# Layer 1 of a four-layer image network: one matrix for a patch's own pixels, filtered pixels only at patch edges, two channels side by side

## The chip, the cores and the metric

The kernel runs on one core of a Trainium2 chip. A core has TensorE for matrix products (PE in the profile, with its weight loads as PEld), VectorE (DVE), ScalarE (ACT), GpSimd (POOL) and SyncE (SP), which here does nothing but issue DMAs. The engines run their own instruction streams in order and wait for each other on semaphores. On-chip memory (SBUF) has 128 partitions; products land in PSUM banks of 128 x 512 fp32. The metric is the device time of one execution in microseconds.

## The reference

Four residual layers work on four images of 48 x 256 x 256, fp32, each after a group normalisation. Layer 1 is the one that is edited:

```python
y = jnp.einsum('oc,bchw->bohw', w_in, x)                    # 48 -> 288 channels
yp = y.reshape(B, C2, ht, P, wt, P).transpose(0, 1, 2, 4, 3, 5)
f = jnp.fft.rfft2(yp) * fft_mask[None]                      # patches of 8 x 8
yp = jnp.fft.irfft2(f, s=(P, P))
y = yp.transpose(0, 1, 2, 4, 3, 5).reshape(B, C2, H2, W2)
y = lax.conv_general_dilated(y, w_dw, ..., feature_group_count=C2)   # depthwise 3 x 3
x1, x2 = jnp.split(y, 2, axis=1)
g = jax.nn.gelu(x1, approximate=False) * x2
return jnp.einsum('oc,bchw->bohw', w_out, g)                # 144 -> 48 channels
```

Layer 0 has 1x1 and depthwise convolutions and a product of spectra; layer 2 samples an integral image at four computed corners of each pixel (gathers from DRAM); layer 3 has convolutions, a gate and a spectral filter.

## The kernel before, in words

**Two streams.** `run` interleaves two generators, a and b, by the costs that they yield (`yield 12` and so on, one unit is meant as about 1 us): the one that is behind goes on. Stream a does layers 0 and 1 of image 0, then of images 1, 2 and 3, then layer 3 of all four. Stream b does the first statistics of each image, once the weights of layer 1 (`patch_weights`, after the first statistics of image 0), and then layer 2 of image after image. Layer 2 of an image needs its layer 1. So layer 1 of image 0 runs with nothing beside it, and layer 1 of images 1 to 3 beside layer 2 of the image before. Stream a issues its DMAs on SyncE, stream b on GpSimd; layer 2's loads A and B of shifted rows go out on ScalarE. Stream a has five PSUM banks, stream b two.

**Layer 1 in three stages.** A tile of 8 x 16 pixels (two patches) is laid over the 128 partitions. The first stage makes the 288 channels and stores them in DRAM (`hD`). The second, which is edited, goes over 72 groups of four channels. The third reads the gated product (`gD`) by strips, transposes it and projects it to 48 channels.

**A group of the second stage, before.** A filter by spectrum on a tile is a 128 x 128 matrix for each channel (`cD`). The depthwise convolution is another matrix, 128 + 52 rows by 128 (`tD`): 128 rows for the tile's own pixels, 52 for the pixels of other tiles around it. `fetch` loads the next group: `hg` (pixels, 1 MB), `ct` (filter), `tt` (own rows of the depthwise matrix), `ht` (its 52 halo rows). `filtered(c)` makes the filtered pixels of a channel (L728) and ACT or DVE copies them into `ys`, four channels one behind the other, with an empty row and column around them. `gated(c)`, one group later, makes each output channel by two products into one bank: own pixels `ys` with `tt` (L741), then halo pixels `yh` with `ht` (L742, 65 rows). ACT takes the gelu of one channel and DVE multiplies it with its partner (L746). The order of products in a group is filtered 0, 1; gated 0, 2; filtered 2, 3; gated 1, 3.

The halo `yh` is gathered by eight DMAs from SBUF to SBUF (L783): for each entry of `AROUND`, some partitions of `ys`, shifted along the free dimension, go to others. Two entries have 16 partitions, two 8 and four (the corners) one. A copied partition holds four channels, 8976 bytes. `gD` is written every second group (L787). `ys` and `yh` have two buffers each, `hg` and `ct` two, `tt` and `ht` three.

The order in which SyncE issues per group is: `hg`, `ct`, `tt`, `ht` of the next group, eight copies `yh` of this group, and in every second group `gD`.

Of the kernel before, what the change touches and what calls it, by code (L numbers as in the profile page):

```python
# [8 lines left out]
F32 = mybir.dt.float32  # L9
I32 = mybir.dt.int32  # L10
AF = mybir.ActivationFunctionType
ALU = mybir.AluOpType
# [7 lines left out]
NS = 16  # L20
# [6 lines left out]
NG = 72  # L27
GROUPS = [c + 144 * h for g in range(NG) for h in range(2) for c in (2 * g, 2 * g + 1)]

YW = 17  # L30
YC = 33 * YW
Y0 = YW + 1
YL = Y0 + 4 * YC + Y0


AROUND = [
    (0, 16, 112, 1, -YW), (16, 16, 0, 1, YW), (32, 8, 15, 16, -1), (40, 8, 0, 16, 1),
    (48, 1, 127, 1, -YW - 1), (49, 1, 112, 1, -YW + 1), (50, 1, 15, 1, YW - 1), (51, 1, 0, 1, YW + 1),
]
NH = 52  # L40

NZ = 65

# [143 lines left out]
class Net:  # L189
# [430 lines left out]
    def patch_weights(self):  # L620


        nc, a = self.nc, self.a
        self.cD = self.dram.tile([NG, 128, 4, 128], F32, name="cD")[:]
        self.tD = self.dram.tile([4 * NG, (128 + NH) * 128], F32, name="tD")[:]
        with ExitStack() as ctx:
            w = ctx.enter_context(self.pool("pw", 1))
            sb = ctx.enter_context(self.pool("pb", 2))
            mask = self.filter_mask(a["L1_fft_mask"], [(0, 4 * NG)], w)
            dw = w.tile([9, 4 * NG], F32, name="dw")  # L630
            self.dma(dw[:], a["L1_w_dw"])
            for g in range(NG):
                m = sb.tile([128, 4, 128], F32, name="m", tag="m")
                for c in range(4):
                    nc.vector.tensor_scalar(
                        m[:, c, :], self.ri, mask[:, 4 * g + c : 4 * g + c + 1], None, ALU.mult
                    )
                ps = self.bank()
                nc.tensor.matmul(ps[:], self.ri, m[:].rearrange("p c k -> p (c k)"), start=True, stop=True)
                ct = sb.tile([128, 512], F32, name="ct", tag="ct")  # L640
                nc.scalar.copy(ct[:], ps[:])
                self.dma(self.cD[g].rearrange("p c k -> p (c k)"), ct[:])
                yield 3
            for q0 in range(0, (128 + NH) * 128, 4608):
                sh = sb.tile([9, 4608], F32, name="sh", tag="sh")
                self.dma(sh[:], a["c_shift"][:, q0 : q0 + 4608])
                for c0 in range(0, 4 * NG, 96):
                    tt = sb.tile([96, 4608], F32, name="tt", tag="tt")
                    for q in range(0, 4608, 512):
                        ps = self.bank()  # L650
                        nc.tensor.matmul(ps[:96, :], dw[:, c0 : c0 + 96], sh[:, q : q + 512], start=True, stop=True)
                        if q % 1024:
                            nc.vector.tensor_copy(tt[:, q : q + 512], ps[:96, :])
                        else:
                            nc.scalar.copy(tt[:, q : q + 512], ps[:96, :])
                    self.dma(self.tD[c0 : c0 + 96, q0 : q0 + 4608], tt[:])
                    yield 12

    def layer1(self, x, mr, y):
        nc, a = self.nc, self.a  # L660
# [3 lines left out]
        with ExitStack() as ctx:  # L664
            w = ctx.enter_context(self.pool("wa", 1))
            sb = ctx.enter_context(self.pool("ba", 2))
# [24 lines left out]
            for s in range(NS):  # L691
                xp = xps[s % 2]
                hs = sb.tile([128, 4 * NG, 2, 16], F32, name="hs", tag="hs")
                for b in range(16):
                    for h in range(2):
                        ps = self.bank()
                        nc.tensor.matmul(  # L697
                            ps[:, :288], xp[64 * h : 64 * h + 48, b, :], win[64 * h : 64 * h + 48],
                            start=True, stop=True,
# [11 lines left out]
        with ExitStack() as ctx:  # L711
            w = ctx.enter_context(self.pool("wb", 1))
            sb = ctx.enter_context(self.pool("bb", 2))
            ys = [w.tile([128, YL], F32, name=self.nm("ys")) for _ in range(2)]
            yhs = [w.tile([NZ, YL], F32, name=self.nm("yh")) for _ in range(2)]
            hts = [w.tile([NZ, 4, 128], F32, name=self.nm("ht")) for _ in range(3)]
            for t in ys + yhs + hts:
                nc.vector.memset(t[:], 0.0)

            pick = lambda t, k, c: t[:k, Y0 + YC * c : Y0 + YC * c + 32 * YW].rearrange(  # L720
                "p (h s b) -> p s h b", h=2, b=YW
            )[:, :, :, :16]
            order = lambda t: t.rearrange("p (s h b) -> p s h b", h=2, b=16)
            todo, gt = None, None

            def filtered(c):
                ps = self.bank()
                nc.tensor.matmul(  # L728
                    ps[:].rearrange("p (s n) -> p s n", n=32), ct[:, c, :], hg[:, :, c, :], start=True, stop=True
                )  # L730
                if c % 2:
                    nc.vector.tensor_copy(pick(yt, 128, c), order(ps[:]))  # L732
                else:
                    nc.scalar.copy(pick(yt, 128, c), order(ps[:]))

            def gated(c):
                go, yo, yho, to, ho = todo
                both = []
                for q in (c, c + 2):
                    ps = self.bank()  # L740
                    nc.tensor.matmul(order(ps[:]), to[:, q, :], pick(yo, 128, q), start=True, stop=False)  # L741
                    nc.tensor.matmul(order(ps[:]), ho[:, q, :], pick(yho, NZ, q), start=False, stop=True)  # L742
                    both.append(ps)
                gl = sb.tile([128, 512], F32, name="gl", tag="gl")
                nc.scalar.activation(gl[:], both[0][:], AF.Gelu)
                nc.vector.tensor_mul(  # L746
                    gt[:, :, 2 * (go % 2) + c, :], gl[:].rearrange("p (s n) -> p s n", n=32),
                    both[1][:].rearrange("p (s n) -> p s n", n=32),
                )


            def fetch(g):
                hg = sb.tile([128, NS, 4, 32], F32, name="hg", tag="hg")
                self.dma(hg[:].rearrange("p s c n -> p s (c n)"), hD[:, g])
                ct = sb.tile([128, 4, 128], F32, name="ct", tag="ct")
                self.dma(ct[:], self.cD[g])
                tt = sb.tile([128, 4, 128], F32, name="tt", tag="tt", bufs=3)
                ht = hts[g % 3]
                tv = self.tD[4 * g : 4 * g + 4].rearrange("c (k m) -> k c m", m=128)
                self.dma(tt[:], tv[:128])  # L760
                self.dma(ht[:NH], tv[128:])
                return hg, ct, tt, ht

            fetched = {0: fetch(0)}
            for g in range(NG + 1):
                if g < NG:
                    yt = ys[g % 2]
                    if g + 1 < NG:
                        fetched[g + 1] = fetch(g + 1)
                    hg, ct, tt, ht = fetched.pop(g)  # L770
                if todo is not None and todo[0] % 2 == 0:
                    gt = sb.tile([128, NS, 4, 32], F32, name="gt", tag="gt")
                for c in range(2):
                    if g < NG:
                        filtered(2 * c)
                        filtered(2 * c + 1)
                    if todo is not None:
                        gated(c)
                if g < NG:
                    yh = yhs[g % 2]  # L780
                    n = YL - 2 * Y0
                    for k, m, p0, dp, far in AROUND:
                        self.dma(  # L783
                            yh[k : k + m, Y0 : Y0 + n], yt[p0 : p0 + (m - 1) * dp + 1 : dp, Y0 + far : Y0 + far + n]
                        )
                if todo is not None and todo[0] % 2:
                    self.dma(gD[:, :, todo[0] // 2, :], gt[:].rearrange("p s c n -> p s (c n)"))  # L787
                todo = (g, yt, yh, tt, ht)
                yield 12
        st = self.stat.tile([CP, 129, 6], F32, name=self.nm("st"), tag="st" + self.stream, bufs=1)  # L790
        with ExitStack() as ctx:
            w = ctx.enter_context(self.pool("wc", 1))
            sb = ctx.enter_context(self.pool("bc", 2))
# [42 lines left out]
            strips, xts, last = {}, {}, None  # L836
# [535 lines left out]
```

## Time and profile before

| what | us |
|---|---|
| median of 3 runs | 20871.12 (20867.39 to 20881.85) |
| the profiled execution's own time | 20882.08 |
| its span, first to last instruction | 20880.3 |
| L728, filtered pixels: 2304 instructions, busy | 1264.4 |
| L741, own pixels: 2304, busy | 1174.1 |
| L742, halo: 2304, busy | 1163.1 |
| L732 and L734, evictions on DVE and ACT, busy | 396.7 and 346.2 |
| idle TensorE before L728, of it until `ct<-cD` | 417.5, 339.5 |
| idle TensorE before L742, of it until `yh<-ys` | 145.7, 111.6 |

A product of fp32 with 512 columns stands as two instructions, so 288 groups with four products a line give 2304. The profile records one execution; a row has an instruction's line, engine, operation, tiles and shape, how many there were, their busy time and mean, and how long the engine was idle before them and what ended that. DMAs are issued through a helper, so that they all have its line, L227, and are told apart by their tiles.

### The profile page before, as it was taken

The page shows a single profiled execution, that of the slowest core. Times are in us where ns is not written, and L with a number is a line of the kernel's source. Part 1 is how long each engine was busy: PE and PEld are TensorE (multiplying, and loading weights), DVE is VectorE, ACT ScalarE, POOL GpSimd, SP SyncE. Part 2 cuts the span into 40 slices and gives each one's busy share as a digit, 9 for nine tenths or more (in the row PEclk, how much of TensorE's full clock was granted, in tenths as well). Part 3 has the DMA queues.
Part 4 walks back from the last instruction along what each step waited for, and adds up shares of the span by engine and source line. Part 5 has one row for each costly group of instructions (what it writes and reads, how often), then busy time and mean ns, then how long its engine had stood idle before and what let it go on. Part 6 is the DMA issues. An engine that isn't in the chain of part 4 may idle for free.

```text
span 20880.3 us, 231985 instructions
## 1 busy us (share of the span) xinstructions
PE 18892.3 (90%) x79032; PEld 12001.4 (57%) x79032; DVE 10763.0 (52%) x21931; ACT 5909.3 (28%) x12275; POOL 8637.2 (41%) x8887
## 2 busy tenths in 40 slices
PE   7998798999878989998788899997888999999999
PEld 4565435666533346665433466654334787878888
DVE  4544322477765534677645447776554255555521
ACT  2333312344321123443311234433112211111111
POOL 1000000277754511777555216775552066666600
PEclk9899799999968999999689899996899999999999
DMA  4623886555588975555889755558897566666633
GB/s 114 135 55 82 233 217 194 137 132 134 132 235 230 241 207 139 130 134 127 233 230 240 219 133 130 133 127 229 236 239 225 137 150 151 158 152 160 151 76 74
DMA packets 2444896, 3440.27 MB, mean 165 GB/s; under 512 B 580102, under 2 KB 1997038, under 8 KB 2333179
## 3 DMA queue, kind: packets, MB, share of 16 engines
q1 hardware_dynamic: 1908216, 2084.50, 38.2%
q0 software_dynamic: 452560, 1110.45, 21.1%
q10 hardware_dynamic: 82944, 230.48, 4.4%
q8 instruction: 635, 10.40, 0.2%
q14 instruction: 541, 4.43, 0.1%
HBM read 2486.99 MB, written 802.77 MB: 158 GB/s over the span
## 4 chain that ended last, share of the span: by engine, by line
PE 65%; DMA 15%; DVE 7%; POOL 7%; issue 4%; SPq 1%; ACT 1%; DVEq 0%; ACTq 0%; POOLq 0%
PE ps L427 19%; POOL V L1037 7%; PE ps L947 6%; PE ps L728 5%; PE ps L435 4%; PE ps L741 4%; DMA ct<-cD 4%; PE ps L742 3%; PE ps L697 3%; PE ps L828 3%; DMA hD<-hs 2%; PE ps L1188 2%; DVE V L1050 2%; PE ps L815 1%; PE ps L966 1%
## 5 line engine op out<-in xcount | busy, mean ns | idle before, releaser
L1037 POOL DMA_INDIRECT V<-t,idx x8192 | 8227.0, 1004 | 4897.9 <-issue 2346.8
L427 PE MATMUL ps<-W,A 128*128 128x288 f32 (+1 forms) x24576 | 5547.3, 374 | 85.9 <-DMA A<-x 23.4
L427 PEld LDWEIGHTS ps<-W,A 128*128 128x128 f32 x24576 | 4281.6, 191 | 1226.6 <-issue 523.4
L227 POOL DMA_DIRECT2D X<-x x192 | 144.5, 757 | 4302.6 <-DMA x<-xt 3040.1
L1050 DVE TENSOR_TENSOR V<-V 128x1536 f32<-128x1536 f32 (+3 forms) x2048 | 1839.3, 900 | 19.2
L1048 DVE TENSOR_TENSOR V<-V,w 128x3072 f32<-128x3072 f32 x512 | 1713.3, 3346 | 35.9 <-DMA V<-t,idx 27.0
L728 PE MATMUL ps<-hg,ct 128*128 128x512 f32 x2304 | 1264.4, 676 | 417.5 <-DMA ct<-cD 339.5
L947 PE MATMUL ps<-A,W 112*96 112x512 f32 x3072 | 1544.9, 642 | 26.2 <-DVE xt L1069 21.5
L697 PE MATMUL ps<-win,xp 48*128 48x288 f32 x4096 | 1054.8, 594 | 547.9 <-DVE xp L684 232.4
L508 ACT COPY qkv<-ps 128x288 f32<-128x288 f32 x2048 | 769.9, 400 | 2641.1 <-PE ps L427 1258.4
L435 PE MATMUL ps<-W,B 58*128 58x288 f32 (+1 forms) x8192 | 1271.5, 391 | 26.1 <-DMA B<-x 13.8
L742 PE MATMUL ps<-yh,ht 65*128 65x512 f32 x2304 | 1163.1, 649 | 145.7 <-DMA yh<-ys 111.6
L531 DVE BATCH_NORM_STATS2 bs<-ps 128x6 f32<-128x96 f32 x2048 | 397.4, 251 | 1634.3 <-PE ps L529 1632.3
L741 PE MATMUL ps<-ys,tt 128*128 128x512 f32 x2304 | 1174.1, 632 | 27.6 <-DVE ys L732 25.7
L697 PEld LDWEIGHTS ps<-win,xp 48*128 48x128 f32 x4096 | 647.3, 259 | 924.3 <-ACT hs L704 291.9
L1168 DVE TENSOR_TENSOR gp<-gl,ps 128x192 f32<-128x192 f32 x1024 | 353.8, 351 | 1588.1 <-ACT gl L1167 1579.9
L728 PEld LDWEIGHTS ps<-hg,ct 128*128 128x128 f32 x2304 | 468.0, 211 | 1051.6 <-issue 949.1
L1167 ACT ACTIVATE gl<-ps 128x192 f32<-128x192 f32 x1024 | 332.7, 330 | 2529.4 <-PE ps L427 2245.4
L435 PEld LDWEIGHTS ps<-W,B 58*128 58x128 f32 x8192 | 762.4, 186 | 454.1 <-issue 346.4
L746 DVE TENSOR_TENSOR gt<-gl,ps 128x512 f32<-128x512 f32 x576 | 395.1, 687 | 1142.2 <-PE ps L742 1136.6
L947 PEld LDWEIGHTS ps<-A,W 112*96 112x96 f32 x3072 | 513.9, 176 | 731.4 <-issue 690.3
L742 PEld LDWEIGHTS ps<-yh,ht 65*128 65x128 f32 x2304 | 451.3, 199 | 794.3 <-issue 699.4
(186 smaller groups left out, 24654.4 us busy)
## 6 DMA issues: line engine op xcount, KB each, us to landing
hD<-hs SPq DMA_DIRECT2D x64, 4608.0 KB
hg<-hD SPq DMA_DIRECT2D x288, 1024.0 KB
gD<-gt SPq DMA_DIRECT2D x144, 1024.0 KB
gs<-gD SPq DMA_DIRECT2D x64, 2304.0 KB
V<-t,idx POOLq DMA_INDIRECT x8192
A<-x SPq DMA_DIRECT2D x512, 193.5 KB
xt<-x SPq DMA_DIRECT2D x256, 387.0 KB
A<-x ACTq DMA_DIRECT2D x512, 193.5 KB
```

The source lines that it names most:

```text
L427: nc.tensor.matmul(to(q, b), A[:, r + q, 128 * b + g : 128 * b + g + 128], W[:, g, :], start=b == 0 and g == 0, stop=b == 1 and g == 2,)
L435: nc.tensor.matmul(to(q, b), B[p, r // 2, 128 * b : 128 * b + 128], W[p, 3, :], start=b == 1, stop=b == 0)
L508: nc.scalar.copy(t.qkv[:, 2 * q + b, :], banks[2 * b + q][:, 0:288])
L697: nc.tensor.matmul(ps[:, :288], xp[64 * h : 64 * h + 48, b, :], win[64 * h : 64 * h + 48], start=True, stop=True,)
L728: nc.tensor.matmul(ps[:].rearrange("p (s n) -> p s n", n=32), ct[:, c, :], hg[:, :, c, :], start=True, stop=True)
L741: nc.tensor.matmul(order(ps[:]), to[:, q, :], pick(yo, 128, q), start=True, stop=False)
L742: nc.tensor.matmul(order(ps[:]), ho[:, q, :], pick(yho, NZ, q), start=False, stop=True)
L828: nc.tensor.matmul(pp[:CP, :], pr[:, q, :], got[q][:], start=q == 0, stop=q == 2)
L947: m = nc.tensor.matmul(ps[:96, :].rearrange("p (r c) -> p r c", c=256), W[: kk[g], g, :], of[: kk[g]], start=g == 0, stop=g == 3,)
L1037: nc.gpsimd.indirect_dma_start(out=V[:, k, 4 * cr : 4 * cr + 4, :].rearrange("p e c -> p (e c)"), out_offset=None, in_=table, in_offset=ba ...
L1048: self.pinned(nc.vector.tensor_mul(Vm, Vm, wm.unsqueeze(2).to_broadcast([128, 64, 48])))
L1050: nc.vector.tensor_add(V[:, :, 0:n, :], V[:, :, 0:n, :], V[:, :, n : 2 * n, :])
```

## The change

The filter and the own rows of the depthwise matrix of a channel are multiplied once, in `patch_weights`, to one 128 x 128 matrix. With it stand 52 columns of the filter (in 64), those that give the filtered pixels which other tiles need (`fD`, 4 x 192 columns a group). In the second stage `around` makes filtered pixels for these 64 columns only, two channels side by side: channel c on PSUM partitions 0 to 63 and channel c + 2 on 64 to 127, so that `ye` holds four channels in the width of two. `gated`, one group later, makes the own part straight from the unfiltered `hg` and adds the halo part, 52 rows at partition 0 or 64. Each group has four products with 64 columns, four with 128 on 128 rows and four with 128 on 52 rows. The halo copies become sixteen, half as many bytes each. `hg` and `f` have three buffers. In `patch_weights` the loop over the groups comes behind the making of `tD`, which it reads.

```diff
-YL = Y0 + 4 * YC + Y0
+YL = Y0 + 2 * YC + Y0
+NF = 128 + 64
...
+            for g in range(NG):
+                own = sb.tile([128, 4, 128], F32, name="own", tag="own")
+                self.dma(own[:], self.tD[4 * g : 4 * g + 4].rearrange("c (k m) -> k c m", m=128)[:128])
...
+                f = fs[g % 2]
+                for k, n, p0, dp, far in AROUND:
+                    nc.vector.tensor_copy(
+                        f[:, :, 128 + k : 128 + k + n], ct[:, :, p0 : p0 + (n - 1) * dp + 1 : dp]
+                    )
+                ps = self.bank()
+                for c in range(4):
+                    nc.tensor.matmul(
+                        ps[:, 128 * c : 128 * c + 128], ct[:, c, :], own[:, c, :], start=True, stop=True
+                    )
+                nc.scalar.copy(f[:, :, 0:128], ps[:].rearrange("p (c k) -> p c k", k=128))
+                self.dma(self.fD[g], f[:].rearrange("p c k -> p (c k)"))
+                yield 5
...
-            def filtered(c):
+            def around(c):
                 ps = self.bank()
-                nc.tensor.matmul(
-                    ps[:].rearrange("p (s n) -> p s n", n=32), ct[:, c, :], hg[:, :, c, :], start=True, stop=True
-                )
-                if c % 2:
-                    nc.vector.tensor_copy(pick(yt, 128, c), order(ps[:]))
+                for q in range(2):
+                    nc.tensor.matmul(
+                        strips(ps[64 * q : 64 * q + 64, :]), f[:, c + 2 * q, 128:NF], hg[:, :, c + 2 * q, :],
+                        start=True, stop=True,
+                    )
+                if c:
+                    nc.vector.tensor_copy(pick(ye, slice(0, 128), c), order(ps[:]))
...
+            def gated():
+                go, hgo, fo, yho, ho = todo
                 both = []
+                for c in range(2):
+                    both.append([self.bank() for _ in range(2)])
+                    for q in range(2):
+                        nc.tensor.matmul(
+                            strips(both[c][q][:]), fo[:, c + 2 * q, 0:128], hgo[:, :, c + 2 * q, :],
+                            start=True, stop=False,
+                        )
+                for c in range(2):
+                    for q in range(2):
+                        rows = slice(64 * q, 64 * q + NH)
+                        nc.tensor.matmul(
+                            order(both[c][q][:]), ho[rows, c, :], pick(yho, rows, c), start=False, stop=True
+                        )
...
             def fetch(g):
-                hg = sb.tile([128, NS, 4, 32], F32, name="hg", tag="hg")
+                hg = sb.tile([128, NS, 4, 32], F32, name="hg", tag="hg", bufs=3)
                 self.dma(hg[:].rearrange("p s c n -> p s (c n)"), hD[:, g])
-                ct = sb.tile([128, 4, 128], F32, name="ct", tag="ct")
-                self.dma(ct[:], self.cD[g])
-                tt = sb.tile([128, 4, 128], F32, name="tt", tag="tt", bufs=3)
+                f = sb.tile([128, 4, NF], F32, name="f", tag="f", bufs=3)
+                self.dma(f[:].rearrange("p c k -> p (c k)"), self.fD[g])
                 ht = hts[g % 3]
-                tv = self.tD[4 * g : 4 * g + 4].rearrange("c (k m) -> k c m", m=128)
-                self.dma(tt[:], tv[:128])
-                self.dma(ht[:NH], tv[128:])
+                for q in range(2):
+                    self.dma(
+                        ht[64 * q : 64 * q + NH],
+                        self.tD[4 * g + 2 * q : 4 * g + 2 * q + 2].rearrange("c (k m) -> k c m", m=128)[128:],
+                    )
...
                     for k, m, p0, dp, far in AROUND:
-                        self.dma(
-                            yh[k : k + m, Y0 : Y0 + n], yt[p0 : p0 + (m - 1) * dp + 1 : dp, Y0 + far : Y0 + far + n]
-                        )
+                        for q in (0, 64):
+                            self.dma(
+                                yh[q + k : q + k + m, Y0 : Y0 + n], ye[q + k : q + k + m, Y0 + far : Y0 + far + n]
+                            )
```

## The prediction, made before the run

> **What bounds it now.** I read the page first, its busy shares and its chain of waits:
>
> ```profile
> PE 18892.3 (90%) x79032; PEld 12001.4 (57%) x79032; DVE 10763.0 (52%) x21931; ACT 5909.3 (28%) x12275; POOL 8637.2 (41%) x8887
> ...
> PE 65%; DMA 15%; DVE 7%; POOL 7%; issue 4%; SPq 1%; ACT 1%; DVEq 0%; ACTq 0%; POOLq 0%
> ```
>
> TensorE is 90% busy and holds 65% of the chain, so fewer matmuls look like time. But 15% of the chain is DMA, and the largest DMA entry there is `ct<-cD`, in the very stage that is edited. So the stage must be read alone. The rows of `hg<-hD` begin at 2345, 6262, 10464 and 14669 us: 72 groups for each of the four images. The windows view over these stretches (us, then busy of PE, weight load, DVE, ACT, POOL; granted clock; DMA share; GB/s):
>
> ```profile
> 2345.00:3211.00 866.00, 795.67 (x1668) 331.81 (x1669) 200.81 (x285) 168.62 (x280) 0.00 (x0) 0.93 0.80 217
> 6262.00:7398.00 1136.00, 991.87 (x2287) 422.78 (x2288) 590.88 (x874) 189.55 (x312) 597.95 (x632) 0.90 0.91 238
> 10464.00:11605.00 1141.00, 989.01 (x2284) 423.49 (x2285) 589.50 (x872) 189.57 (x312) 597.91 (x632) 0.89 0.90 236
> 14669.00:15793.00 1124.00, 979.16 (x2290) 418.69 (x2291) 590.55 (x874) 189.58 (x312) 597.18 (x630) 0.91 0.91 240
> ```
>
> One group costs 12.2 us in image 0, where stream b is idle, and 16.0 us in images 1 to 3 beside layer 2 (71 steps from the first `hg` to the last); together 4267 us. The view has no column for SyncE, which only issues DMAs. Its timeline over two groups of image 0:
>
> ```profile
> 2818.84 0.45 SPq L227 DMA_DIRECT2D hg<-hD  x1
> 2819.34 0.42 SPq L227 DMA_DIRECT2D ct<-cD  x1
> 2819.86 0.38 SPq L227 DMA_DIRECT2D tt<-tD  x1
> 2820.34 0.84 SPq L227 DMA_DIRECT2D ht<-tD  x1
> 2821.28 7.46 SPq L227 DMA_DIRECT2D yh<-ys  x8
> 2828.91 0.60 SPq L227 DMA_DIRECT2D gD<-gt  x1
> 2829.61 1.88 SPq L227 DMA_DIRECT2D hg<-hD  x1
> 2831.55 1.22 SPq L227 DMA_DIRECT2D ct<-cD  x1
> 2832.86 0.59 SPq L227 DMA_DIRECT2D tt<-tD  x1
> 2833.54 0.60 SPq L227 DMA_DIRECT2D ht<-tD  x1
> 2834.24 9.23 SPq L227 DMA_DIRECT2D yh<-ys  x8
> 2843.58 0.46 SPq L227 DMA_DIRECT2D hg<-hD  x1
> ```
>
> From `hg` to `hg` this is 10.8 and 14.0 us, and SyncE is issuing in nearly all of it: 23.7 of 24.7 us. The eight `yh` copies take 7 to 9 us of each group. **SyncE's queue is as full as TensorE**, and in this stage it is the tighter of the two. What one copy costs it, by the rows of `yh`:
>
> ```profile
> L227 SPq DMA_DIRECT2D yh<-ys x2304: 554/712/2864, 2357.8 to 15812.8; - x192
> ```
>
> The median is 0.71 us, the minimum 0.55. The single rows of the trace split it by shape: 16 partitions 0.58 us, 8 partitions 0.61, one partition (a corner) 0.73. So 144 KB cost less than 9 KB: it is a price for each DMA, not for its bytes. `ct` and `tt`, 256 KB each, have medians of 0.44 and 0.39.
>
> A second rule sits on the same queue. The DMAs that SyncE and ScalarE issue share eight completion semaphores in turn, and each waits until the DMA eight places before it on its semaphore has landed. In the quiet group above `hg` lands 5.1 us after its issue, `ct` 0.7 us later, `tt` 2.2 us after that and `ht` 1.2 us after that (semaphore events); the fifth to eighth `yh` go out just behind those four landings.
>
> **The change, part by part.**
>
> *TensorE, per group.* Before: 12 products, each two instructions at some 0.445 us start to start (4 of L728 take 1.72 us in the chain), 10.7 us. After: 4 own products 3.56 us; 4 halo products on 52 rows at partitions 0 and 64, alternating; 4 products with 64 columns. For alternating row halves the trace has L435 beside L427 (start, us, what):
>
> ```profile
> 4500.08 1.24 PE L435 MATMUL ps<-W,B 58*128 58x288 f32 x8
> 4501.25 3.18 PE L427 MATMUL ps<-W,A 128*128 128x288 f32 x12
> ```
>
> 0.155 against 0.265 us each, a factor 0.585, so the halo costs 8 x 0.445 x 0.585 = 2.1 us. No row shows a column pair. Bounds: 2.1 us if it overlaps as the row halves do, 3.6 if not. The Trainium skill (TensorEngine Tiling, Theoretical Speedup) promises up to 2x for both; the clock gate page (TensorE: Matmul & The Clock Gate, The mechanism) says that weights load beside a running matmul only where the row groups differ, which speaks against the column pair. I take 3.6. Sum 9.3 us, 1.4 saved (2.9 at best). This is worth nothing unless TensorE ends the group.
>
> *DVE and ACT.* Two of four evictions of 0.69 and 0.60 us go, 1.3 us a group, not on the path (DVE 23% and ACT 19% busy in image 0). They now end early in the group, so the copies no longer wait for the last of four.
>
> *Bytes.* `ct` 256 + `tt` 256 KB become `f` 384 KB; halo weights and copies keep theirs. 128 of some 2620 KB a group go, 5%. The slow landing of `tt` (2.2 us) goes, `f` adds some 0.35 us.
>
> *SyncE.* Fetches stay four. The eight `yh` copies become sixteen of half the bytes, in the same shapes (16, 8 and 1 partitions): 8 more at 0.71 us and 0.065 us between two, **+6.2 us a group**. Here a rule is weighed. The Trainium skill (DMA: Bandwidth & Descriptors, Issuing engines are not separate DMA queues) says that a sequencer's time to start a DMA is usually small beside the DMA itself. By it only the bytes count: a group gets 5% shorter, 4267 us lose some 200. By the row, sixteen copies need 16 x 0.78 = 12.4 us of one queue, more than a whole group of image 0. The row decides.
>
> I put the issues and landings in order, image 0, from `hg` = 0. Quiet group: `f` 0.5, `ht` 1.0 and 1.5, copies 1 to 4 from 2.0 to 4.0; copy 5 waits for `hg` (5.1), 6 for `f` (6.2), 7 and 8 for the halves of `ht` (6.9, 7.5); the eight corners follow at 0.78 each from 8.2, the end at 14.5. Then `gD`, 0.7. Group after `gD`: `hg` 1.9 and `f` 1.2 us to issue, `hg` landing at 8.5, `f` 9.6, `ht` 10.3 and 11.0, corners from 11.8, end 18.1. The pair is 33.3 us against 24.7. The same reckoning gives 10.8 and 14.0 for before. With 0.2 us of semaphore instructions: **16.8 us a group, +4.6 x 72 = +331 us.**
>
> Images 1 to 3: SyncE issues for 8.9 us a group, needs some 2 us for gaps and semaphore instructions, and waits 5 us. After, issue and gaps alone are 15.5 (uninflated) to 16.4 us, against 16.0 for the whole group now. Of the waits, those for the evictions of `ys` (2.4 us: rows of L732, L728, L741 in its waits) mostly go, those for `hg`, `f` and layer 2's loads `A<-x` (1.4 us before) stay in part; I keep 1.9. **18.3 us, +2.3 x 216 = +497 us.** Bounds: 16.5 (no waits left, +108 us) and 21 (all 5 us stay, +1080).
>
> TensorE needs 9.3 us and some 4 of layer 2 there, and idles more. The next `hg` and the halo's copies come a group ahead, so no other loop closes later than SyncE's.
>
> *Weights, once, beside layer 0 of image 0,* where TensorE is 1812.6 of 1860 us busy, so nothing covers it. 72 groups x 4 products 128x128x128, two instructions each at 0.13 us (L885's size): 75 us. One more ACT copy (0.6 us) and eight small DVE copies (0.17 to 0.2 us each, by the 128x16 rows) a group lie beside TensorE. A second product now waits for ACT's copy of the first, and the load of `own` (512-byte pieces, POOL's queue, behind the previous store) comes two groups ahead. Bounds 60 and 250 us; I take 90, near the work itself.
>
> Sum: 331 + 497 + 90 = 918 on the profiled execution's 20,882 us, 21,800; the median of the runs shown is 11 us below it: **21,790 us.**
>
> **Rivals.** (a) *Faster:* the issue price halves with the bytes (deciding point: a 16-copy set under some 7 us). Then SyncE stays near 10 us and DMA bandwidth ends the group: 0.91 x 16.0 us x 3.69/3.82 = 14.1 us (a group of image 1 moves 3.82 MB in all: 118.34 MB in 31 groups from 6500 to 7000 us), with waits 14.8, in images 1 to 3 (-260), and 11.0 in image 0 (-86); with the weights 20,615. For it: DMA 0.91 busy and less of it. Against: the 9 KB copies that cost more than 144 KB. 5%. (b) *Much slower:* in images 1 to 3 TensorE, idling, is granted less clock (0.65 to 0.75 in neighbouring stretches of 500 us), layer 2's 13 us become 18 and alternate with SyncE's waits: 21 us, +1080, with 331 and 120: 22,400. 7%. (c) *No difference:* the row pairs' gain pays for the queue; needs groups of 14.1 us in images 1 to 3, under SyncE's 15.5. 2%.
>
> **Numbers.** Forecast 86%, its own range 21,400 to 22,150, from the 16.5 and 20 us of images 1 to 3. The range reaches up to (b) in part: 21,370 to 22,300. A measurement here tells 0.2% from no change. Faster 5%, within 0.2% 2%, slower 93%.
>
> **Signs.** Right: sixteen `yh` issues of 0.6 to 0.73 us, SyncE without gaps in image 0, 16 to 17 us from `hg` to `hg` there, and 17 to 20 later; lower PE share and DMA share in these windows; PE waiting for `yh` or `hg`. Wrong: `yh` issues near 0.35 us, groups under 15 us, or a loss that sits in layer 0's weights or outside the four stretches.

## The result and the profile after

The changed kernel takes 22,003.18 us (median of 4 runs, 22,000.82 to 22,034.29), the kernel before 20,869.25 us beside it (20,852.44 to 20,881.85): a ratio of 1.0544, 95% interval 1.0531 to 1.0556. It is 5.4% slower; the prediction was 21,790 us with a range of 21,370 to 22,300.

The page of the changed kernel: busy shares, then the shares of the chain that ended last.

```profile
PE 18771.7 (85%) x79608; PEld 11778.6 (54%) x79608; DVE 10615.9 (48%) x22209; ACT 5776.0 (26%) x12059; POOL 8685.0 (39%) x8959
...
PE 57%; DMA 19%; SPq 8%; DVE 6%; POOL 5%; issue 3%; ACT 1%; ACTq 0%; DVEq 0%; POOLq 0%
```

TensorE is less busy than before and holds less of the chain, 57% against 65%. SyncE's queue (SPq) holds 8% where it had 1%. The windows over the four stretches of the edited stage, with the columns as before (us; busy PE, PEld, DVE, ACT, POOL; granted clock; DMA share; GB/s):

```profile
2397.00:3598.00 1201.00, 770.09 (x1680) 258.77 (x1680) 143.95 (x209) 126.37 (x210) 0.00 (x0) 0.74 0.50 149
6670.00:8044.00 1374.00, 946.70 (x2296) 358.68 (x2296) 545.74 (x801) 147.79 (x242) 599.51 (x634) 0.76 0.67 190
11107.00:12483.00 1376.00, 954.36 (x2296) 361.46 (x2296) 545.98 (x801) 147.79 (x242) 600.32 (x635) 0.75 0.66 190
15548.00:16924.00 1376.00, 945.96 (x2296) 360.13 (x2296) 545.69 (x801) 147.78 (x242) 598.35 (x634) 0.76 0.67 189
```

Each stretch is longer, and everything in it that was nearly full has become emptier: the DMA engines went from 0.80 and 0.91 to 0.50 and 0.67 of their time, TensorE from 795.67 of 866 us to 770.09 of 1201, and the granted clock fell with it. SyncE's timeline shows what is full (start, us, what):

```profile
2805.38 0.43 SPq L227 DMA_DIRECT2D hg<-hD  x1
2805.91 0.37 SPq L227 DMA_DIRECT2D f<-fD  x1
2806.37 1.13 SPq L227 DMA_DIRECT2D ht<-tD  x2
2807.61 13.70 SPq L227 DMA_DIRECT2D yh<-ye  x16
2821.41 0.60 SPq L227 DMA_DIRECT2D gD<-gt  x1
2822.11 1.83 SPq L227 DMA_DIRECT2D hg<-hD  x1
```

From one `hg` to the next it is 16.7 us, and the row of the sixteen copies fills 13.7 of them. Such a row holds short waits between the copies as well: the copies' own durations add up to 10.8 us a group in image 0, and all issues to 13.85 of 16.92 (8.87 of 12.21 before). Most groups alternate: in the median 15.4 us, and 18.7 where `hg` stands behind `gD`. The whole time went like this (rows of `hg`, 71 steps an image, where the prediction counts 72 groups; the rest from the first products of layer 1):

| part | before, us | after, us | measured | predicted |
|---|---|---|---|---|
| stage, image 0 | 866.6 | 1201.6 | +335 | +331 |
| stage, images 1 to 3 | 3401.0 | 4126.1 | +725 | +497 |
| start, layer 0 of image 0, weights | 1982.8 | 2037.3 | +54.5 | +90 |
| all else | | | +5.5 | 0 |
| span | 20,880.3 | 22,000.5 | +1120 | +918 |

### The profile page after: what moved, and what is told of

Its sections match the earlier page's. It is cut to its first block, busy times and chain, and to the rows that moved or that the text cites. A ratio compares the mean times of both kernels' runs of the same rounds, so it can differ in the third digit from the quotient of the medians.

```text
span 22000.5 us, 235878 instructions
## 1 busy us (share of the span) xinstructions
PE 18771.7 (85%) x79608; PEld 11778.6 (54%) x79608; DVE 10615.9 (48%) x22209; ACT 5776.0 (26%) x12059; POOL 8685.0 (39%) x8959
## 4 chain that ended last, share of the span: by engine, by line
PE 57%; DMA 19%; SPq 8%; DVE 6%; POOL 5%; issue 3%; ACT 1%; ACTq 0%; DVEq 0%; POOLq 0%
PE ps L427 19%; SPq L227 8%; DMA f<-fD 7%; PE ps L977 5%; POOL V L1067 5%; PE ps L435 4%; PE ps L715 3%; PE ps L858 3%; PE ps L1218 2%; DMA ht<-tD 2%; DMA hD<-hs 2%; DMA yh<-ye 2%; PE ps L773 2%; DVE V L1080 1%; PE ps L845 1%
## 5 line engine op out<-in xcount | busy, mean ns | idle before, releaser
L751 PE MATMUL ps<-hg,f 128*64 128x512 f32 x2304 | 922.2, 928 | 1166.5 <-DMA f<-fD 1021.0
L977 PE MATMUL ps<-A,W 112*96 112x512 f32 x3072 | 1640.6, 676 | 25.7 <-DVE xt L1099 22.5
L773 PE MATMUL ps<-yh,ht 52*128 52x512 f32 x2304 | 1024.8, 807 | 673.5 <-DMA yh<-ye 599.1
L766 PE MATMUL ps<-hg,f 128*128 128x512 f32 x2304 | 1162.5, 650 | 0.0
L751 PEld LDWEIGHTS ps<-hg,f 128*64 128x64 f32 x2304 | 219.8, 192 | 1709.0 <-issue 1551.0
L773 PEld LDWEIGHTS ps<-yh,ht 52*128 52x128 f32 x2304 | 379.8, 225 | 1184.3 <-issue 905.8
L778 ACT ACTIVATE gl<-ps 128x512 f32<-128x512 f32 x576 | 344.0, 597 | 2493.9 <-PE ps L773 2481.0
L1197 ACT ACTIVATE gl<-ps 128x192 f32<-128x192 f32 x1024 | 333.4, 331 | 2532.8 <-PE ps L427 2225.4
```

The costliest lines, as they stand in the source:

```text
L751: nc.tensor.matmul(strips(ps[64 * q : 64 * q + 64, :]), f[:, c + 2 * q, 128:NF], hg[:, :, c + 2 * q, :], start=True, stop=True,)
L766: nc.tensor.matmul(strips(both[c][q][:]), fo[:, c + 2 * q, 0:128], hgo[:, :, c + 2 * q, :], start=True, stop=False,)
L773: nc.tensor.matmul(order(both[c][q][:]), ho[rows, c, :], pick(yho, rows, c), start=False, stop=True)
L977: m = nc.tensor.matmul(ps[:96, :].rearrange("p (r c) -> p r c", c=256), W[: kk[g], g, :], of[: kk[g]], start=g == 0, stop=g == 3,)
```

## The experiments

The chips were of two kinds. On one kind the kernel before takes 20,850 to 20,880 us, on the other 25,350 to 25,384. On the second kind image 0 runs like on the first (10.89 and 10.85 us a group for the last variant below, which ran on both), but all that runs beside layer 2 later is slower, also parts that nobody edited (layer 0 of image 1 took 2795 us in the first experiment below, 2169 in the profile of before). Why is open. So image 0 is compared between all runs, images 1 to 3 only within a kind.

### The kernel before, with sixteen copies

```diff
-                        self.dma(yh[k : k + m, Y0 : Y0 + n], yt[..., Y0 + far : Y0 + far + n])
+                        for i in (Y0, Y0 + n // 2):
+                            self.dma(yh[k : k + m, i : i + n // 2], yt[..., i + far : i + far + n // 2])
```

> The kernel before, with each of its eight halo copies cut in two along the channels: the same bytes, the same products, sixteen DMAs. Theory (SyncE pays for each DMA, whatever its bytes): eight more issues of some 0.69 us and gaps of 0.065, 6 us of SyncE's queue a group; image 0 goes from 12.2 to about 17 us a group, images 1 to 3 from 16.0 to about 19.5 to 20.5, the whole to about 22,100 us (21,800 to 22,300). Rival 1 (bytes and DMA bandwidth end the group) and rival 2 (the loss sits in the new products and their lower clock): both leave this kernel at about 20,870 us with groups of 12.2 and 16.0 us.

Measured: 26,196.9 us beside 25,384.39, ratio 1.032 (1.0303 to 1.0338), second kind of chip. Image 0 went from 12.2 to 18.0 us a group, 5.8 more. A line of its windows view and one of SyncE's timeline:

```profile
2354.00:3634.00 1280.00, 940.74 (x1680) 364.93 (x1680) 202.18 (x287) 169.30 (x281) 0.00 (x0) 0.80 0.54 147
```

```profile
2795.27 13.58 SPq L227 DMA_DIRECT2D yh<-ys  x16
```

The products, bytes, fetches and weights are those of the kernel before, only each copy is cut in two; the copies take 13.58 us of SyncE as in the changed kernel, TensorE's clock falls from 0.93 to 0.80, and the DMA share from 0.80 to 0.54. So doubling the number of DMAs makes the loss by itself in image 0, and both rivals fall there. The whole change loses 4.7 us a group: what else it does gives back about one. Over all images the loss is smaller than expected, 812 us where 22,100 meant some 1,230. Image 0 has 414 of them; for images 1 to 3 there is no trace of the kernel before on such a chip, so where the rest is missing stays open.

### The changed kernel, with copies an eighth as long

```diff
-                    n = YL - 2 * Y0
+                    n = (YL - 2 * Y0) // 8
```

> The changed kernel with its sixteen halo copies, each cut to an eighth of its length, which leaves out seven eighths of the halo pixels: the same number of DMAs, some 410 KB of 2.5 MB a group less. Theory (price for each DMA): the copies still cost 0.6 to 0.7 us of SyncE each; about 21,850 us (21,650 to 22,000), 16 to 17 us a group in image 0; what is gained comes from hg and f landing a little earlier in images 1 to 3. Rival (bytes): an issue falls under 0.4 us or the stage shrinks with its bytes by a sixth, under 21,300 us.

Measured: 25,786.91 us, ratio 1.0163 (1.0146 to 1.018), on the second kind of chip, so the total can't be set against the numbers expected. Image 0: 16.34 us a group against 16.92. Its timeline:

```profile
2796.09 0.48 SPq L227 DMA_DIRECT2D hg<-hD  x1
2796.67 0.36 SPq L227 DMA_DIRECT2D f<-fD  x1
2797.12 1.06 SPq L227 DMA_DIRECT2D ht<-tD  x2
2798.27 12.73 SPq L227 DMA_DIRECT2D yh<-ye  x16
```

Seven eighths of the halo's bytes are gone, and sixteen copies still take 12.73 us. In the single rows the medians of image 0 are 0.58 us for 16 partitions, 0.62 to 0.68 for 8 and 0.73 to 0.78 for a corner, to 0.01 us the same as in the full copies. Between these two lengths SyncE's price is for the DMA and its shape, not for its bytes. In images 1 to 3 the bytes may count for something: groups take 19.4 us there, and 20.6 with full copies in the order of the next but one experiment, on the same chip; no run tells the order from the bytes.

### The changed kernel, with half of the copies

```diff
-                        for q in (0, 64):
+                        for q in (0,):
```

> The changed kernel with only the eight copies of partitions 0 to 63, which leaves out the halo of channels c + 2: the same products. Theory (SyncE's queue ends the group): 5.5 to 6 us of it go in every group; image 0 about 11 us a group, images 1 to 3 about 14, the whole about 20,430 us (20,200 to 20,700), under the kernel before. Rival 1 (bandwidth): 9% of the stage's bytes go, at most 9% of its 5,330 us, not under 21,500 us. Rival 2 (the waits for hg and f end the group, not the issues): about 21,900 us.

Measured: 24,994.95 us, ratio to the kernel before 0.9854 (0.9835 to 0.9873), second kind of chip: 389 us under it where the expectation has some 440. Image 0: 11.3 us a group (11 expected). The rival of the waits falls, and with it that of bandwidth, which left the kernel some 600 us above the kernel before; the DMA engines' share in image 0 even rises from 0.50 to 0.63 though there is less to move.

### Another order of the same DMAs

```diff
                 self.dma(hg[...], hD[:, g])
+                copies(4)
                 self.dma(f[...], self.fD[g])
                 for q in range(2):
+                    copies(4)
                     self.dma(ht[64 * q : 64 * q + NH], ...)
...
+                copies(16)
```

The call of `fetch` with these lines moves behind `gated`, to where the copies are issued.

> The changed kernel with the same 20 or 21 DMAs a group in another order on SyncE: hg of the next group, four copies, f, four copies, the first half of ht, four copies, the second half, four copies; so the semaphore of hg or f comes round some 5 us after their issue and not after four quick ones. Theory (what is left of SyncE's time beside its issues, 1.8 us a group in image 0 and 4 in images 1 to 3, is waiting for the landing of hg, f and ht eight places earlier): most of these waits go, 0.5 and 1.5 us stay; about 21,370 us (21,200 to 21,600), image 0 about 15.6 and images 1 to 3 about 17 us a group. Rival (that time is for PSUM banks, layer 2's loads or DMA bandwidth, and turns up at the next instruction): 21,950 to 22,050 us.

> The changed kernel with its DMAs in the spread order, once more, since images 1 to 3 of the first time can't be set against the changed kernel on that chip. The first time gave 16.6 us a group in image 0, 0.35 less than the changed kernel where 1.3 was expected. Theory (waits for the landings of hg, f, ht fill the rest of SyncE's time in images 1 to 3): still 2 to 2.5 us a group less there, about 21,450 us on a chip like that of the result. Rival, now the likelier (the rest moves to the next instruction that needs the landing or a PSUM bank): within 0.8 us a group of the changed kernel in images 1 to 3, 21,800 to 21,980 us.

Measured: 26,001.45 us, 1.0238 (1.0221 to 1.0255), and 26,046.15, 1.0274 (1.0256 to 1.0291), both on chips of the second kind. Image 0: 16.57 us a group both times, 0.35 less than the changed kernel and not 1.3. A miss, and the timeline tells why:

```profile
2810.81 0.60 SPq L227 DMA_DIRECT2D gD<-gt  x1
2811.51 1.83 SPq L227 DMA_DIRECT2D hg<-hD  x1
2813.45 3.23 SPq L227 DMA_DIRECT2D yh<-ye  x4
2816.79 0.53 SPq L227 DMA_DIRECT2D f<-fD  x1
2817.36 5.29 SPq L227 DMA_DIRECT2D yh<-ye  x4
```

Other blocks of four copies take 2.5 to 3.2 us; the one here takes 5.29, because the eighth DMA after `hg` stands in it and waits for `hg`. By the semaphore events `hg`, issued behind `gD`, landed 9.8 us after its issue began (8.2 in the changed kernel, 5.0 there without `gD`), and the DMA eight places on was ready after 7.3. The wait for `f` is gone from SyncE's waits (52.6 us in image 0), those for `hg` rose from 70.0 to 89.0, and others took the rest: 192 us of waits in all became 181. For images 1 to 3 (20.6 us a group) there is no run of the changed kernel on such a chip, so whether the order is worth anything there stays open.

### Half of the copies on ScalarE, in both kernels

```diff
-                            self.dma(
+                            (nc.scalar if q else nc.sync).dma_start(
                                 yh[q + k : q + k + m, Y0 : Y0 + n], ye[...]
```

> The changed kernel with the eight copies to partitions 64 to 127 issued by ScalarE, the others by SyncE: same bytes, same products. Theory (SyncE's queue ends the group): SyncE issues for some 8.3 us a group in place of 14; image 0 about 11.5 us a group (11 to 12.5), images 1 to 3 3.5 to 5 us a group less than the changed kernel on the same chip, in all 1,100 to 1,400 us less than it, which is at or somewhat under the kernel before. Rival 1 (bytes): no difference from the changed kernel. Rival 2 (the copies stand before the gelu in ScalarE's order and hold up the PSUM banks): at most 500 us less than the changed kernel, TensorE waiting for banks that ScalarE frees.

In the kernel before, four of its eight go to ScalarE:

```diff
-                        self.dma(
+                        (nc.scalar if m == 8 or k in (48, 50) else nc.sync).dma_start(
                             yh[k : k + m, Y0 : Y0 + n], yt[...]
```

> The kernel before with four of its eight halo copies issued by ScalarE. Theory: SyncE is as full as TensorE in its groups, so this helps a little, until TensorE (10.7 us a group) or the DMA engines (0.91 busy in images 1 to 3) end the group: image 0 from 12.2 to about 11.2, images 1 to 3 from 16.0 to about 15.5 on the chip of the result; 100 to 250 us under the kernel before. Rival (TensorE alone bounded the kernel before): within 40 us of it, 12.2 us a group in image 0.

And the changed kernel again, beside these two:

> The changed kernel itself once more, as a yardstick for the other runs beside it, since the chip of the first experiments took 25,384 us for the kernel before, 22% longer than the chip of the result. Theory (the loss is SyncE's time in 288 groups): image 0 16.9 us a group, and on whatever chip a loss of 900 to 1,200 us in all; on a chip like that of the result 22,000 us. Rival (the loss is a share of the whole, by a lower clock): 5.4% on any chip, 1,370 us where the kernel before takes 25,384.

Measured, on one chip of the first kind: the changed kernel 21,986.31 us (1.0538, 1.0521 to 1.0556), with two queues 21,434.25 (1.028, 1.0263 to 1.0297), the kernel before with two queues 21,127.5 (1.0124, 1.0107 to 1.0141). The changed kernel gains 552 us, half of what was expected, 15.15 us a group in image 0. That is near the number of the second rival (at most 500 us), but its reason is the smaller part: TensorE waited 58.7 us for gelus in image 0, and 333.4 us for `f`. The kernel before *loses* 273 us, which neither theory had: 13.8 us a group in image 0 in place of 12.2, though SyncE issues for 5.5 us of it in place of 8.9. The waits (what waits, for what: us in total, times, longest), first of the changed kernel with two queues, then of the kernel before with two queues, both in image 0:

```profile
SPq L227 <- DMA yh<-ye: 354.9, 82, 9.9
...
ACT gl L778 <- DMA yh<-ye: 472.1, 48, 12.2
...
PE ps L751 <- DMA f<-fD: 333.4, 62, 25.8
```

```profile
SPq L227 <- DMA yh<-ys: 494.1, 135, 8.2
```

In the kernel before with two queues SyncE waits half of the stretch for landings of `yh`. The eight completion semaphores (108 to 115 in the trace) go round over the DMAs of both queues in program order, so SyncE's fetch of the next group stands behind a copy that ScalarE has yet to issue, behind its own evictions and gelus; and a gelu stands behind the copies. A new wait took the place of the issues. So the theory, put as "SyncE's issue time ends the group", was too narrow: fewer microseconds on SyncE help only if the DMAs do not come later for it. This reading rests on the waits; no run gave the two queues semaphores of their own. And as this chip was of the first kind again, the rival of the last expectation, a loss of 5.4% on any chip, was not put to the test.

### Copies for two groups at once

`ye` and `yh` hold the four channels of each of two groups and are twice as wide; every second group issues sixteen copies, and `gated` runs two groups after `around`, with four buffers of `hg`, `f` and `ht` and one of `gt`. `gD` goes out in the middle of the copies.

```diff
-                todo = (g, hg, f, yh, ht)
+                todo.append((g, hg, f, yh, ht))
...
-                if g < NG:
+                if g < NG and g % 2:
                     n = YL - 2 * Y0
                     for k, m, p0, dp, far in AROUND:
+                        if k == 32 and g > 2:
+                            self.dma(gD[:, :, (g - 2) // 2, :], gt[...])
                         for q in (0, 64):
                             self.dma(yh[q + k : q + k + m, Y0 : Y0 + n], ye[...])
```

> The changed kernel with its halo copies made for two groups at once: sixteen copies of double length in every second group, eight a group as before the change, the same bytes; gated runs two groups after around instead of one. Theory (price for each DMA): SyncE needs about 20 us for two groups and 2 to 4 of waits; image 0 about 11.2 us a group (10.5 to 12.5), images 1 to 3 3 to 5 us a group less than the changed kernel on the same chip, in all 900 to 1,400 less than it: about the kernel before or somewhat under it. Rival (bytes): no difference from the changed kernel, the copies of double length cost SyncE double.

Measured: 21,319.92 us, ratio 1.0221 (1.0204 to 1.0238), 666 under the changed kernel on that chip, less than expected: 14.5 us a group in image 0 and 16.6 in images 1 to 3. SyncE issues for 8.65 us a group but stands still for most of the rest. A copy of double length takes 0.86 us of it, not double the 0.68 of the changed kernel. SyncE's waits in image 0, and TensorE's for the copies:

```profile
SPq L227 <- DVE ye L756: 169.5, 35, 6.5
SPq L227 <- DVE gt L779: 130.0, 34, 4.5
...
PE ps L773 <- DMA yh<-ye: 305.1, 34, 9.4
```

The burst of copies waits for the second group's evictions, the halo products of two groups wait for the burst, and the next `around` stands behind them on TensorE: a loop that no queue's length shows.

### Eight strided copies

The last variant keeps all halo pixels. In each block of 64 partitions the 16 rows of an entry lie at every 4th partition, the 8 rows at every 8th and a corner once, so step times rows is 64, and one DMA with that step runs through both blocks:

```diff
 AROUND = [
-    (0, 16, 112, 1, -YW), (16, 16, 0, 1, YW), (32, 8, 15, 16, -1), ...
+    (0, 4, 16, 112, 1, -YW), (1, 4, 16, 0, 1, YW), (2, 8, 8, 15, 16, -1), ...   # k, step, m, ...
...
-NH = 52
+NH = 64
...
-                        f[:, :, 128 + k : 128 + k + n], ct[...]
+                        f[:, :, 128 + k : 128 + k + (n - 1) * step + 1 : step], ct[...]
...
-                        for q in (0, 64):
-                            self.dma(yh[q + k : q + k + m, ...], ye[q + k : q + k + m, ...])
+                        rows = slice(k, k + (2 * m - 1) * step + 1, step)
+                        self.dma(yh[rows, Y0 : Y0 + n], ye[rows, Y0 + far : Y0 + far + n])
```

The halo rows of the depthwise matrix are numbered in the same way; 12 of the 64 rows are zero.

> The changed kernel with the halo rows of each block of 64 partitions laid out in steps (16 rows every 4th, 8 rows every 8th, a corner once in 64), so that one DMA fetches the same shift for both channels of a pair: eight copies a group instead of sixteen, all halo pixels and all bytes as in the changed kernel, with 64 halo rows (12 of them zero) in place of 52. Theory (SyncE pays for each DMA): 5.5 to 6 us of its queue go in every group; image 0 about 11.5 us a group, images 1 to 3 about 14.6 (13.9 to 15.5, where the DMA engines' bandwidth begins to end the group); in all about 1,400 us less than the changed kernel, 20,560 (20,400 to 20,800) on a chip like that of the result: under the kernel before. Rival 1 (bytes or descriptors): a copy of 32 rows costs SyncE double and nothing is gained. Rival 2 (DMA bandwidth ends the group of images 1 to 3 at the 16 us of the kernel before): about 20,880, no better than it.

> The changed kernel with eight strided halo copies a group, once more beside the changed kernel on one chip. The first time gave 0.978 of the kernel before, 10.9 us a group in image 0 and 16.7 in images 1 to 3, on a chip where the kernel before took 25,350 us. Theory (price for each DMA): on a chip like that of the result 20,400 to 20,700 us, under the kernel before, groups of 10.9 and 14 to 15; on the other kind of chip again 0.975 to 0.982 of the kernel before and 3 to 4 us a group under the changed kernel in images 1 to 3. Rival (the gain over the kernel before exists only where layer 2 is slow beside it): 20,850 us or more on a chip like that of the result.

> The changed kernel, a third time, as the yardstick for the experiments on chips where the kernel before takes about 25,350 us. On such a chip: theory (SyncE's groups): image 0 16.9 us a group; images 1 to 3 about 19.5 to 21 us a group, near the spread order's 20.6 if the order does nothing, 2 us above it if waits for landings were taken away by it; in all 600 to 1,000 us over the kernel before. On a chip like that of the result: 22,000 us and 19.4 us a group.

Measured: on the second kind of chip 24,839.63 us, ratio 0.9784 (0.9767 to 0.9801). On one chip of the first kind the kernel before 20,877.90, the changed kernel 22,041.77 (1.0558, 1.0541 to 1.0574) and this one **20,269.21 us, 0.9708 (0.9694 to 0.9721)**: 3% faster than the kernel before, 1,773 us under the changed kernel. Its windows in images 0 and 1:

```profile
2407.00:3178.00 771.00, 595.96 (x1668) 201.00 (x1670) 143.24 (x208) 125.65 (x209) 0.00 (x0) 0.88 0.72 234
6236.00:7177.00 941.00, 746.63 (x2284) 283.56 (x2286) 535.50 (x795) 146.43 (x241) 606.75 (x621) 0.90 0.91 277
...
```

10.85 us a group in image 0 and 13.2 to 13.4 in images 1 to 3, some 6.1 less than the changed kernel in both. SyncE's timeline:

```profile
2801.70 0.33 SPq L228 DMA_DIRECT2D hg<-hD  x1
2802.13 0.38 SPq L228 DMA_DIRECT2D f<-fD  x1
2802.60 1.38 SPq L228 DMA_DIRECT2D ht<-tD  x2
2804.43 4.88 SPq L228 DMA_DIRECT2D yh<-ye  x8
2810.70 0.60 SPq L228 DMA_DIRECT2D gD<-gt  x1
```

The copies cost 4.2 us of SyncE a group where the sixteen cost 10.8: 5.5 us because there are eight fewer, 1.1 because they are cheaper, a corner for two partitions 0.47 to 0.51 us against 0.74 to 0.78 for one. The gain over the kernel before is larger than expected, since images 1 to 3 were put at 14.6 us a group, where DMA bandwidth was to end them.

## Why the prediction was right, and where it was not

**What bounds the stage: right.** The loss sits in the four stretches, 1,060 of 1,120 us. The kernel before with sixteen copies makes it in image 0 without any of the other edits; copies an eighth as long hardly lessen it; eight strided copies turn it into a gain. SyncE's issues grew by 5.0 us a group in image 0, from 8.87 to 13.85, and the group by 4.7. One reading on the way was too strong: that SyncE was issuing in 23.7 of 24.7 us before counts the waits inside the rows of `yh` as issues. It issued for 8.87 of 12.21 us, and TensorE was fuller (795.67 of 866 us). That SyncE's chain of issues and waits nonetheless left no room shows in the kernel before with sixteen copies, where some 5.5 more microseconds of issues and gaps made the group 5.8 longer.

**The price of a copy: right.** 0.71 us each was taken, and 0.065 between two; the mean of the sixteen is 0.68 to 0.69. The row of the copies in the changed kernel (count: minimum, median, maximum in ns):

```profile
L227 SPq DMA_DIRECT2D yh<-ye x4608: 507/738/2622, 2407.5 to 16953.9; - x192
```

The rule that was weighed against it, the Trainium skill's (DMA: Bandwidth & Descriptors, Issuing engines are not separate DMA queues), has the time to start a DMA as usually small beside the DMA. It does not hold for these copies: a corner takes 0.74 us to issue and has landed 1.9 us after the issue began, and twenty issues are 14 of the group's 16.9 us.

**Image 0: right,** 16.8 us a group expected and 16.9 measured, and by the way that was worked out: in the group shown, the fifth, sixth and seventh copy go out 5.0, 6.3 and 7.9 us after `hg`, each just behind the landing of `hg`, `f` and the first half of `ht` (5.1, 6.2 and 6.9 in the working), and the two kinds of group take 15.4 and 18.7 us where it had 15.2 and 18.1.

**Images 1 to 3: two terms were mis-sized, and their errors cancel in part.** The 18.3 us were 16.4 of issues and gaps and 1.9 of waits. Issues are 14.2 us a group in image 1 and the 20 to 21 gaps some 1.3, together 15.5, the lower of the prediction's two figures; so 3.9 of the 19.4 us are waits, twice the 1.9. The step that failed is "those for `hg`, `f` and layer 2's loads `A<-x` (1.4 us before) stay in part; I keep 1.9". SyncE's waits in image 1, first of the kernel before, then of the changed kernel (us in total for 71 steps, times, longest):

```profile
SPq L227 <- DMA A<-x: 97.8, 22, 14.5
SPq L227 <- DVE ys L732: 90.7, 43, 7.7
SPq L227 <- DMA tt<-tD: 63.1, 43, 2.9
SPq L227 <- DMA ct<-cD: 55.4, 34, 5.1
SPq L227 <- DMA hg<-hD: 54.9, 32, 4.5
...
SPq L227 <- DMA ht<-tD: 25.1, 25, 7.3
```

```profile
SPq L227 <- DMA hg<-hD: 105.0, 62, 5.5
SPq L227 <- DMA f<-fD: 75.9, 56, 5.9
SPq L227 <- PE ps L773: 48.0, 50, 2.6
SPq L227 <- DMA A<-x: 40.0, 13, 7.7
SPq L227 <- DMA ht<-tD: 30.4, 22, 5.1
```

(The view counts a wait from the end of the issue before it, gap included, so its sum, 4.8 us a group, is above 3.9.) Before the change the waits for the landing of the fetches (`hg`, `ct`, `tt`, `ht`) were 198.5 us; now (`hg`, `f`, `ht`) they are 211.3. They did not stay in part but in full. What went is what was said to go, the waits for the evictions of `ys` and their products (171.7 to 11.2 us), and more than half of those for `A<-x` (97.8 to 40.0). New are 48.0 us for the halo products (8.0 before), 0.7 a group (0.8 in image 0), a wait for TensorE that the prediction had put at nothing. At the size that the trace of before gave them, 2.8 us for fetches and 1.4 for `A<-x`, the waits would have been 4.2 and the group 19.7 with the 15.5. The prediction gave no row for keeping less than half of them, and that was the error. That 4.2 comes near is in part luck: `A<-x` fell to 0.6 us, and the halo products took its place.

**TensorE: the right number for the wrong reason.** The page's rows of the products of 64 columns (L751) and of the halo (L773):

```profile
L751 PE MATMUL ps<-hg,f 128*64 128x512 f32 x2304 | 922.2, 928 | 1166.5 <-DMA f<-fD 1021.0
...
L773 PE MATMUL ps<-yh,ht 52*128 52x512 f32 x2304 | 1024.8, 807 | 673.5 <-DMA yh<-ye 599.1
```

Both wait for DMAs that SyncE issued late. A column pair was taken to run one after the other, 3.6 us a group, and in the changed kernel eight take 3.57 to 3.68. But in the run with strided copies (L752 there) the same eight take two times in turn:

```profile
2800.13 3.51 PE L752 MATMUL ps<-hg,f 128*64 128x512 f32 x8 [4.76 <-DMA f<-fD]
2803.57 3.78 PE L767 MATMUL ps<-hg,f 128*128 128x512 f32 x8
2807.28 2.05 PE L774 MATMUL ps<-yh,ht 64*128 64x512 f32 x8
2809.26 1.94 PE L752 MATMUL ps<-hg,f 128*64 128x512 f32 x8
2811.13 3.70 PE L767 MATMUL ps<-hg,f 128*128 128x512 f32 x8
```

and the windows view of that run over the two blocks of 64 columns has the granted clock (the last figure but two) at 0.53 and 1.00:

```profile
2800.10:2803.60 3.50, 3.47 (x9) 0.86 (x9) 0.00 (x0) 0.60 (x1) 0.00 (x0) 0.53 0.37 85
...
2809.30:2811.10 1.80, 1.80 (x10) 0.44 (x8) 1.17 (x2) 1.20 (x2) 0.00 (x0) 1.00 0.04 15
```

So column pairs do overlap, 0.24 us an instruction at full clock; in the changed kernel they come after an idle stretch and at half the clock (0.50 to 0.52 over three such blocks). What the prediction took from the Trainium skill's clock page (TensorE: Matmul & The Clock Gate, The mechanism) is a sentence on weight loads; that a column pair therefore runs one after the other was the prediction's own step, and it failed. The up to 2x of the other page (TensorEngine Tiling, Theoretical Speedup) agrees with this trace: 1.94 us for eight against 3.70 with 128 columns right behind them. The row pairs came as worked out, 2.05 us for eight where 2.1 was taken. The values did not enter the sum, since SyncE ended the group.

**Weights: too high.** 54.5 us in place of 90. TensorE's busy time up to the end of layer 0 rose by 58 us (1812.56 to 1870.70), and its idle time there did not (47 and 46 us). The added products took less than the 75 us worked out, and the delays that the rest of the 90 allowed for (a product that waits for ACT, the load of `own`) did not show. These 35 us too much hide a part of the 228 too little in images 1 to 3.

**The rivals.** (a) fell with the short copies, and its end by DMA bandwidth with the strided ones: 13.3 us a group where it had 14.1. (b) was there in part: the clock fell to 0.76 in image 1, and about as many TensorE instructions are busy for 946.70 us (x2296) as take 746.63 (x2284) with strided copies. How much of the 48 us of waits for L773 comes from it was not tried. (c) did not occur.

## What to carry to other kernels

Where a loop issues many small DMAs from one engine, count the issues a step and multiply by their row in the trace before looking at bytes or TensorE: an edit that kept the bytes of the copies and doubled their number lost 5.4% here. Keep a wait that a row shows at its size unless the edit takes away what is waited for. Lay data out so that one access pattern with a step reaches all pieces of the same shift. Moving DMAs to another engine was no substitute here, where completion semaphores are shared in turn: what the DMAs then wait for is the other engine's order of work.

## What the runs showed of the hardware that was not expected

- A copy of one partition is dearer to issue than one of two, though it moves half: 0.74 us against 0.47. In the trace's operands the row of 4488 bytes of one partition stands as 11 pieces of 408 bytes, with two partitions as whole rows of 4488. Whether the pieces make the price was not tried.
- A DMA share of 0.91 is not by itself an end: the kernel before moved 238 GB/s at that share in image 1, the kernel with strided copies 277 at the same.
- The price of an issue is not quite free of what is queued: `hg` takes 0.33 to 0.48 us of SyncE, and mostly 1.6 to 1.9 right behind `gD`. In the kernel with copies for two groups the copies of 8 partitions, which come behind `gD` there, take 1.36 us in the median, against 0.61 for the same size and shape in the kernel before.
